# Layer 1's product A X in Strassen's form, and the last image's layer 3 by halves of its positions

## The chip, the cores and the metric

The kernel runs on one core of a Trainium2 chip. TensorE (PE) does the matrix products and transposes into eight PSUM banks of 128 x 512 fp32. VectorE (DVE), ScalarE (ACT) and GpSimd (POOL) do the elementwise work, and SyncE (SP) issues most of the transfers. The metric is the device time of one execution in microseconds (us). Three executions of the kernel before gave a median of 2748.43 us.

## The reference

Two images of 512 channels and 32 x 32 = 1024 positions go through four layers, all in fp32. Layer 0 is deformable attention and an MLP, and is not touched here. The others, in short (X is one image, 512 x 1024):

```
# layer 1: linear attention, then batch norm over both images
K, Q, V = Wq X + bq, Wk X + bk, Wv X + bv      # 8 heads of 64
M   = K V^T per head;  Out = Wo (M^T Q) + bo + X
x   = (Out - mean(Out)) * rsqrt(var(Out) + eps) * gamma + beta
# layer 2: non-local attention, mid = 128
f, g = relu(bn(wf x)), relu(bn(wg x));  h = wh x + bh
z    = softmax(f^T g / sqrt(mid)) h^T;  x = wv z + bv + x
# layer 3: rank-one attention with a channel gate
th, ph, g = theta x, phi x, g x                # one row of 1024 each
y    = softmax(th_i * ph_j, over j) . g        # 1024 values
W_y  = bn(W y + b);  gate = sigmoid(se2 relu(se1 mean(x)))
out  = gate * W_y + x
```

## The kernel before, in words

The channels lie on the partitions in KC = 4 groups of 128. `x` and `x2` are SBUF tiles of 128 x 4 x 2048, where the last axis holds both images. The instructions are written for a Tile scheduler: it puts the instructions of each engine in one order and inserts semaphores where data need them. Instructions given to `tc.keep_in_program_order` keep their written order; of the layers shown here the kernel before uses it nowhere. An engine works through its queue strictly in order, and so does SP's queue of transfers. A PSUM or SBUF pool with `bufs=n` hands out n buffers per tag, and the next user waits for the readers of the one it gets.

**Layer 1 (lines 1205 to 1370).** The layer is linear but for the batch norm, so the kernel folds it. It forms the Gram matrix G = X X^T of each image (lines 1225 to 1254: transposes by PE, copies by DVE and ACT in turn, matmuls), U = G Wv^T (L1270 on), M (L1283 on), R and a bias (L1307 on), and at last A = 512 x 512 for each image (`pa`, L1336, copied to SBUF in L1339). The output is A X + bias1 + X. The weights lie in `lw` (Wq, Wv, Wk, and Wo in two forms). Product A X (lines 1340 to 1354): for each output group o and each 512 positions t, four matmuls over k go into one PSUM bank `pr`, and one DVE instruction (L1352) adds bias1 and X and writes `x2`. This gives 64 matmuls of 128 x 128 by 128 x 512. In the profile an fp32 matmul is two records. Banks come from two pools of four (`dps`, `dpg`).

**Batch norm (lines 1357 to 1370).** For each k: four statistics of 128 x 512 (L1360), an aggregate (L1362), small steps with a square root on ACT (L1365), and a normalisation of 128 x 2048 by DVE (L1370). The statistics of a group can run as soon as its outputs of both images are there; the order of outputs is by o, so groups 0 to 2 are normalised while the product still runs.

**Layer 2 (`l2_fg`, `l2_h`, `l2_attn`, `l2_out`).** For each image: f and g (`pf`, L1385, relu on ACT), h by tiles of 128 positions (`ph`, L1404), then for eight tiles t the scores (L1418, two banks), the row maximum on DVE (L1429), the exponential on ACT (L1432), a scaling on DVE (L1434), eight transposes by PE (L1438) and two copies by ACT (L1439). Then z in two halves (`pz`, L1447) and eight outputs (`pr`, L1458), added to x by DVE (L1466), which also sums each group for the gate's mean.

**Layer 3 (`l3_scores`, `part`, `l3_out`).** The three rows are made by matmuls with 32-wide weights into four partition blocks (`prow`, L1479), copied to SBUF (L1486), and spread over the partitions by matmuls (`pp`, L1494). ACT copies phi and g with their bias to `pg` (L1501), DVE takes the extremes of phi (L1505, L1506), PE turns theta into columns (L1510). For each tile of 128 positions `part` does one exponential on ACT (L1527) and one weighted sum on DVE (L1535). `l3_out` forms y, the gate, spreads y over the partitions (`py`, L1572), and writes each output group: o = 0 by DVE (L1583) then ACT (L1584), the others by ACT (L1586) then DVE (L1587), 1024 positions each, with one store of 512 KB for each (L1588). Image 0's layer 3 is interleaved with image 1's layer 2; image 1's comes after it alone, from a pool of four double banks opened when the others are closed.

## Time and profile before

| what | us |
|---|---|
| median of three executions (2748.21 to 2750.68) | 2748.43 |
| the profiled execution | 2746.91 |
| its span, first to last instruction | 2745.1 |
| its mean granted PE clock, full speed = 1 | 0.995 |
| the product A X, PE | 54.95 |
| last product's end to the first score of layer 2, image 0 | 2565.9 to 2580.0 |
| first score of image 0 to its `pz` | 31.7 |
| last output of layer 2, image 1, on DVE | 2709.4 |
| first exponential of the last layer 3 | 2718.11 |
| last DVE instruction | 2741.0 |

A line of the chain gives a start, a length, an engine, the PSUM or SBUF tile and the source line, with the number of records. A line of groups gives line, engine, operation, output and inputs with their shape, then the total busy time, the mean of one in ns, and the idle time just before with what ended it. A line of windows gives, for a stretch, the busy time and the number of instructions of each engine and the granted PE clock.

### The profile page before, as it was taken

The page shows a single profiled execution, that of the slowest core. Times are in us where ns is not written, and L with a number is a line of the kernel's source. Part 1 is how long each engine was busy: PE and PEld are TensorE (multiplying, and loading weights), DVE is VectorE, ACT ScalarE, POOL GpSimd, SP SyncE. Part 2 cuts the span into 40 slices and gives each one's busy share as a digit, 9 for nine tenths or more (in the row PEclk, how much of TensorE's full clock was granted, in tenths as well). Part 3 has the DMA queues.
Part 4 walks back from the last instruction along what each step waited for, and adds up shares of the span by engine and source line. Part 5 has one row for each costly group of instructions (what it writes and reads, how often), then busy time and mean ns, then how long its engine had stood idle before and what let it go on. Part 6 is the DMA issues. An engine that isn't in the chain of part 4 may idle for free.

```text
span 2745.1 us, 49805 instructions
## 1 busy us (share of the span) xinstructions
PE 2693.7 (98%) x19846; PEld 1003.0 (37%) x19846; DVE 2262.8 (82%) x2465; ACT 1540.5 (56%) x1902; POOL 662.2 (24%) x776
## 2 busy tenths in 40 slices
PE   8999999999999999999999999999999999999996
PEld 4343323333332323333333333333444444454543
DVE  7999999999999999999999999999454445523545
ACT  6676677667668766766766776776221111001244
POOL 0333333333333333333333333333100000000000
PEclk9999999999999999999999999999999999999998
DMA  3777777777777777777787788787310000100001
GB/s 122 166 160 159 164 158 157 165 155 159 158 165 153 162 168 154 164 169 155 165 197 163 156 177 186 157 173 158 85 30 23 16 24 23 77 0 1 0 1 62
DMA packets 145479, 335.15 MB, mean 122 GB/s; under 512 B 22592, under 2 KB 32064, under 8 KB 144480
## 3 DMA queue, kind: packets, MB, share of 16 engines
q0 software_dynamic: 77824, 201.38, 41.3%
q1 hardware_dynamic: 66992, 130.08, 13.4%
q8 instruction: 157, 2.57, 0.4%
q14 instruction: 74, 0.61, 0.1%
q10 hardware_dynamic: 432, 0.51, 0.1%
HBM read 58.99 MB, written 4.46 MB: 23 GB/s over the span
## 4 chain that ended last, share of the span: by engine, by line
PE 93%; DVE 4%; ACT 2%; issue 1%; DMA 0%; ACTq 0%; DVEq 0%; POOL 0%; POOLq 0%
PE ph L615 61%; PE A L1098 4%; PE D L1098 4%; PE C L1098 4%; PE po L1033 2%; PE psim L654 2%; PE pr L1345 2%; PE B L1098 2%; DVE h L348 1%; PE pg L1241 1%; PE pa L1336 1%; PE pz L1447 1%; PE pu L1275 1%; PE pscore L1418 1%; DVE r L630 1%
## 5 line engine op out<-in xcount | busy, mean ns | idle before, releaser
L615 PE MATMUL ph<-h,w2a 128*32 128x512 f32 x16384 | 1792.0, 593 | 3.4 <-ACT r L624 3.3
L624 ACT ACTIVATE r<-ph,sb 128x1024 f32<-128x1024 f32 x1024 | 1142.7, 1116 | 546.5 <-PE ph L615 528.1
L348 DVE CUSTOM_DVE_ANT_1 h<-tab 128x1024 f32<-128x1024 f32 x1024 | 1204.1, 1217 | 13.5 <-PE ph L615 10.4
L615 PEld LDWEIGHTS ph<-h,w2a 128*32 128x32 f32 x16384 | 545.1, 109 | 1203.2 <-issue 805.2
L630 DVE SCALAR_TENSOR_TENSOR r<-r,rel,r 128x1024 f32<-128x1024 f32 x512 | 654.5, 1278 | 12.2 <-ACT r L624 11.6
L645 POOL DMA_DIRECT2D xs<-r x512 | 475.5, 1135 | 190.1 <-PE ph L615 94.4
L633 POOL DMA_DIRECT2D r<-r x256 | 221.4, 865 | 1094.2 <-DVE r L630 913.3
L171 ACT ACTIVATE tab<-tab,vec 128x256 f32<-128x256 f32 x252 | 137.1, 544 | 0.0
L1286 POOL MEMSET M<- 128x512 f32 x2 | 1.0, 518 | 442.6 <-DVE x L1162 442.6
L1138 ACT COPY u<-A 128x512 f32<-128x512 f32 x16 | 9.4, 586 | 146.9 <-PE A L1098 146.9
L1117 ACT ACTIVATE h<-h,vec 128x512 f32<-128x512 f32 x32 | 23.1, 721 | 113.6 <-DVE h L1120 113.6
L654 PE MATMUL psim<-xs,cw 128*32 128x512 f32 x512 | 73.7, 592 | 2.0 <-DMA xs<-r 2.0
L1120 DVE TENSOR_TENSOR h<-C,u 128x512 f32<-128x512 f32 x32 | 22.1, 690 | 47.8 <-PE C L1098 47.4
L1098 PE MATMUL A<-xn,w 128*128 128x512 f32 x128 | 60.3, 593 | 0.8 <-DVE x L1040 0.8
L1098 PE MATMUL C<-hT,w 128*128 128x512 f32 x128 | 60.3, 592 | 0.0
L1098 PE MATMUL A<-h,w 128*128 128x512 f32 x128 | 60.1, 592 | 0.0
L1033 PE MATMUL po<-q,vwo 128*128 128x512 f32 x128 | 58.1, 607 | 0.0
L1345 PE MATMUL pr<-x,A 128*128 128x512 f32 x128 | 55.1, 592 | 0.0
L228 DVE SCALAR_TENSOR_TENSOR acc<-q,vec,acc 128x128 f32<-128x128 f32 (+3 forms) x88 | 46.1, 523 | 0.8
L1158 DVE TENSOR_TENSOR x<-D,x 128x512 f32<-128x512 f32 x32 | 22.1, 690 | 25.9 <-PE D L1098 25.9
L850 ACT ACTIVATE e<-e,den 128x64 f32<-128x64 f32 x128 | 41.7, 337 | 2.0 <-DVE den L846 2.0
L1158 DVE TENSOR_TENSOR x<-C,x 128x512 f32<-128x512 f32 x32 | 22.1, 690 | 24.8 <-PE C L1098 24.8
(287 smaller groups left out, 1763.0 us busy)
## 6 DMA issues: line engine op xcount, KB each, us to landing
r<-r POOLq DMA_DIRECT2D x256, 512.0 KB, 4.8
xs<-r SPq DMA_DIRECT2D x512, 128.0 KB, 2.2
xs<-r POOLq DMA_DIRECT2D x512, 128.0 KB, 4.8
tab<-fd SPq DMA_DIRECT2D x63, 512.0 KB, 6.0
lw<-in_l_w_dram SPq DMA_DIRECT2D x5, 1024.0 KB, 8.9
x<-in_x_dram SPq DMA_DIRECT2D x4, 1024.0 KB, 8.6
w<-in_mlp_w_dram SPq DMA_DIRECT2D x8, 512.0 KB, 4.4
w<-in_mlp_w_dram SPq DMA_DIRECT2D x16, 256.0 KB, 3.2
```

The costliest lines, as they stand in the source:

```text
L171: return nc.scalar.activation(tf, tf if src is None else src[:, :, :, ax, :], AF.Identity, bias=0.0 if ax == 0 else v("L0_conv_cpb_b1"), s ...
L228: pin(nc.vector.scalar_tensor_tensor(dst, src, wt_, dst, ALU.mult, ALU.add))
L348: nc.vector._custom_dve(TENSOR_ADD_SAT, out=h1[:, h], in0=tab[:, j, h, 0, :].unsqueeze(1).to_broadcast([P, 32, 32]), in1=tab[:, j, h, 1, : ...
L615: nc.tensor.matmul(ph[t * 32 : (t + 1) * 32, i, :], lhsT=w2a[:, o], rhs=h1s[2 * p + i][:, h, half * 512 : (half + 1) * 512], start=True, s ...
L624: pin(nc.scalar.activation(r, ph, AF.Relu, bias=sb3[:, o, 1:2]))
L630: pin(nc.vector.scalar_tensor_tensor(r0, r1, rel[:, i : i + 1], r0, ALU.mult, ALU.add))
L633: pin(nc.gpsimd.dma_start(rs[p, 0], rs.pop((p, 2)), accum_op=ALU.add))
L645: pin(nc.gpsimd.dma_start(rs[p][i::2], r[i::2, i, :], accum_op=ALU.add))
L654: nc.tensor.matmul(psims[g, kb][m * 32 : (m + 1) * 32, :], lhsT=cw3[:, 3 - i : 35 - i], rhs=rs.pop(p + m), start=(i == 0), stop=(i == 3), ...
L1033: nc.tensor.matmul(po, lhsT=vwo[:, k * B + t // 2, o * P : (o + 1) * P], rhs=q[:, k, ts_], start=(k == 0), stop=(k == KC - 1),)
L1098: nc.tensor.matmul(banks[bank], lhsT=a[an][k], rhs=b_[bn_][k], start=(i < 4 and k == 0), stop=(k == n - 1), skip_group_check=True,)
L1345: nc.tensor.matmul(pr, lhsT=A[b][:, k, o * P : (o + 1) * P], rhs=x[:, k, ns], start=(k == 0), stop=(k == KC - 1),)
```

## The change

The product A X of each image is done by Strassen's seven products (Winograd's form, which the MLP of layer 0 has already). A and X are cut into 2 x 2 blocks: two groups of 128 channels each way, and 512 positions. `xblocks` holds four difference blocks of X (placed in the second image's part of `x2` and in the weights' room for Wq and Wv), formed ahead of R; `ablocks` holds three sums of A and one difference written in place. `layer_out(b, o)` runs the seven products of two matmuls for output group o of each row block; three banks are added into twice or read and filled again, and DVE (ACT for the first) combines them. The loop order is now image, then o, so groups 0 and 2 are complete in both images before 1 and 3. The batch norm goes by these pairs, normalises each image's half separately, and gives one of the eight pieces (image 0, group 1) to ACT. Layer 2's `l2_fg` and `l2_h` add their groups in the order 0, 2, 3, 1.

The second image's layer 3 leaves `l3_scores`, `part` and `l3_out` and becomes `last`, which also holds the last part of layer 2 (`out_z`, `out_x`) and keeps its written order on every engine. Rows, extremes, mean and outputs go by halves of 512 positions. phi and g get their bias already in the copy of the rows and are read from PSUM; y is spread in two parts; the bias of seven of the eight output pieces is added to x ahead by POOL (`raised`), and DVE then does one instruction for each (`final`); the eighth goes by ACT and POOL (`final_act`). There are eight stores of 256 KB. The scheduler's order of image 0's layer 2 also comes out differently.

The diff, cut to its core (functions not shown, such as `out_z` and `theta`, hold the operations of the kernel before on halves):

```diff
@@ -1304,8 +1304,24 @@
+
+        lo, hi = slice(0, 2), slice(2, 4)
+        places = [x2[:, :, HW:], lw[:, 0:2].rearrange("p i k c -> p (i k c)").rearrange("p (n f) -> p n f", n=4)]
+        xblocks = {}
         for b in both:
-            R = d.tile([P, KC, C], F32, name="R")
+            b11, b21, b12, b22 = (
+                x[:, k, b * HW + t * 512 : b * HW + (t + 1) * 512] for t in range(2) for k in (lo, hi)
+            )
+            t1, t2, t3, t4 = (places[b][:, n].rearrange("p (k f) -> p k f", k=2) for n in range(4))
+            nc.vector.tensor_tensor(t1, b12, b11, ALU.subtract)
+            nc.vector.tensor_tensor(t2, b22, t1, ALU.subtract)
+            nc.vector.tensor_tensor(t4, b21, t2, ALU.subtract)
+            nc.vector.tensor_tensor(t3, b22, b12, ALU.subtract)
+            xblocks[b] = {"11": b11, "21": b21, "22": b22, "T1": t1, "T2": t2, "T3": t3, "T4": t4}
...
-            A[b] = d.tile([P, KC, C], F32, name="A")
+            A[b] = d.tile([P, KC, C], F32, name="A", tag="U")
...
-        for o in range(KC):
-            for t in range(NT // 512):
-                b, ns = t // 2, slice(t * 512, (t + 1) * 512)
-                pr = (dps, dpg)[t % 2].tile([P, 512], F32, name="pr", tag="ps g".split()[t % 2])
-                for k in range(KC):
+        ablocks = {}
+        for b in both:
+            a11, a12, a21, a22 = (A[b][:, k, m] for m in (slice(0, C // 2), slice(C // 2, C)) for k in (lo, hi))
+            s1, s2, s4 = (
+                (wk, won)[b][:, n, :].rearrange("p (k f) -> p k f", k=2) for n in range(3)
+            )
+            differences(a11, a21, a12, a22, s1, s2, s4)
+            ablocks[b] = {"11": a11, "12": a12, "S3": a21, "22": a22, "S1": s1, "S2": s2, "S4": s4}
+
+        def layer_out(b, o):
...
+            def plus(to, t, other):
+                nc.vector.tensor_tensor(to, t, other, ALU.add)
+
+            def final(n, t, other):
+                k = 2 * (int(n[0]) - 1) + o
+                nc.vector.scalar_tensor_tensor(at(n, x2), t, bias1[b][:, k : k + 1], other, ALU.add, ALU.add)
+
+            def c1(t):
+                plus(u, t, u)
+                for n in ("22", "21", "12"):
+                    plus(vs[n], u, at(n, x))
+
+            banks = {n: pool.tile([P, 512], F32, name=f"pr{n}", tag=tag) for n in "ABCD"}
+            for i, (bank, an, bn_, read) in enumerate(
+                [
+                    ("A", "11", "11", lambda t: nc.scalar.copy(u, t)),
+                    ("B", "S2", "T2", c1),
+                    ("C", "S3", "T3", lambda t: plus(vs["22"], t, vs["22"])),
+                    ("D", "S1", "T1", lambda t: final("22", t, vs["22"])),
+                    ("A", "12", "21", lambda t: final("11", t, at("11", x))),
+                    ("C", "22", "T4", lambda t: final("21", t, vs["21"])),
+                    ("D", "S4", "22", lambda t: final("12", t, vs["12"])),
+                ]
+            ):
+                for k in range(2):
                     nc.tensor.matmul(
-                        pr,
-                        lhsT=A[b][:, k, o * P : (o + 1) * P],
-                        rhs=x[:, k, ns],
-                        start=(k == 0),
-                        stop=(k == KC - 1),
-                    )
-                nc.vector.scalar_tensor_tensor(
-                    x2[:, o, ns], pr, bias1[b][:, o : o + 1], x[:, o, ns], ALU.add, ALU.add
-                )
+                        banks[bank],
+                        lhsT=ablocks[b][an][:, k, o * P : (o + 1) * P],
+                        rhs=xblocks[b][bn_][:, k, :],
+                        start=(i < 4 and k == 0),
+                        stop=(k == 1),
+                        skip_group_check=True,
+                    )
+                read(banks[bank])
+        for b in both:
+            for o in range(2):
+                layer_out(b, o)
         x = x2
 
-        for k in range(KC):
-            st = d.tile([P, NT // 512, nc.vector.BN_STATS_DIM], F32, name="st", bufs=2)
-            for t in range(NT // 512):
-                nc.vector.bn_stats(st[:, t, :], x[:, k, t * 512 : (t + 1) * 512])
-            mv = d.tile([P, nc.vector.BN_AGGR_DIM], F32, name="mv", bufs=2)
-            nc.vector.bn_aggr(mv, st.rearrange("p t s -> p (t s)"))
-            sc = d.tile([P, 2], F32, name="sc", bufs=2)
-            nc.vector.tensor_scalar(sc[:, 0:1], mv[:, 1:2], EPS, None, ALU.add)
-            nc.scalar.activation(sc[:, 0:1], sc[:, 0:1], AF.Sqrt)
-            nc.vector.reciprocal(sc[:, 0:1], sc[:, 0:1])
-            nc.vector.tensor_tensor(sc[:, 0:1], sc[:, 0:1], v("L1_conv_gamma", k), ALU.mult)
-            nc.vector.tensor_tensor(sc[:, 1:2], mv[:, 0:1], sc[:, 0:1], ALU.mult)
-            nc.vector.tensor_tensor(sc[:, 1:2], v("L1_conv_beta", k), sc[:, 1:2], ALU.subtract)
-            nc.vector.tensor_scalar(x[:, k, :], x[:, k, :], sc[:, 0:1], sc[:, 1:2], ALU.mult, ALU.add)
+        for ks in ((0, 2), (1, 3)):
+            scs = {}
+            for k in ks:
+                st = d.tile([P, NT // 512, nc.vector.BN_STATS_DIM], F32, name="st", bufs=4)
+                for t in range(NT // 512):
+                    nc.vector.bn_stats(st[:, t, :], x[:, k, t * 512 : (t + 1) * 512])
+                mv = d.tile([P, nc.vector.BN_AGGR_DIM], F32, name="mv", bufs=4)
+                nc.vector.bn_aggr(mv, st.rearrange("p t s -> p (t s)"))
+                sc = scs[k] = d.tile([P, 2], F32, name="sc", bufs=4)
+                nc.vector.tensor_scalar(sc[:, 0:1], mv[:, 1:2], EPS, None, ALU.add)
+                nc.scalar.activation(sc[:, 0:1], sc[:, 0:1], AF.Sqrt)
+                nc.vector.reciprocal(sc[:, 0:1], sc[:, 0:1])
+                nc.vector.tensor_tensor(sc[:, 0:1], sc[:, 0:1], v("L1_conv_gamma", k), ALU.mult)
+                nc.vector.tensor_tensor(sc[:, 1:2], mv[:, 0:1], sc[:, 0:1], ALU.mult)
+                nc.vector.tensor_tensor(sc[:, 1:2], v("L1_conv_beta", k), sc[:, 1:2], ALU.subtract)
+            for b in both:
+                for k in ks:
+                    xs = x[:, k, b * HW : (b + 1) * HW]
+                    if (b, k) == (0, 1):
+                        nc.scalar.activation(xs, xs, AF.Identity, bias=scs[k][:, 1:2], scale=scs[k][:, 0:1])
+                    else:
+                        nc.vector.tensor_scalar(xs, xs, scs[k][:, 0:1], scs[k][:, 1:2], ALU.mult, ALU.add)
...
-            for k in range(KC):
+            for j, k in enumerate((0, 2, 3, 1)):
...
+    def last(b, fp, gp, fps, ps, gps, at2, ht):
+
+        pin = tc.keep_in_program_order
+        ve, pe, act = nc.vector, nc.tensor, nc.scalar
...
+        def row(half, k):
+            if k == 0:
+                prow[half] = gps.tile([P, 512], F32, name=f"prow{half}", tag="l3")
+            pin(
+                pe.matmul(
+                    prow[half][k * 32 : (k + 1) * 32, :], lhsT=w3x[:, k, :], rhs=at(k, half), start=True, stop=True
+                )
+            )
+            if k == KC - 1:
+                pin(act.activation(rows3[:, half, :], prow[half], AF.Identity, bias=b3))
+        def spread(half, i):
+            to_all = c("sel3")[:, i : i + 1].to_broadcast([P, P])
+            pin(pe.matmul(pp[i][:, half, :], lhsT=to_all, rhs=rows3[:, half, :], start=True, stop=True))
+        def turn(half):
+            pt[half] = gps.tile([P, 4, P], F32, name=f"ptl{half}", tag="l3")
+            for t in range(4):
+                pin(pe.transpose(pt[half][:, t, :], rows3[:, half, t * P : (t + 1) * P], ident))
+        def extremes(half):
+            pin(ve.tensor_reduce(ext[:, 0, half : half + 1], pp[0][:, half, :], AX.X, ALU.max))
+            pin(ve.tensor_reduce(ext[:, 1, half : half + 1], pp[0][:, half, :], AX.X, ALU.min, negate=True))
+        def weighted(t):
+            e3 = es.pop(t)
+            g3 = pp[1].rearrange("p a n -> p (a n)")
+            pin(ve.scalar_tensor_tensor(e3, e3, 1.0, g3, ALU.mult, ALU.mult, accum_out=nd[:, 0, t : t + 1]))
+        def mean(half):
+            hs = slice(half * 4, half * 4 + 4)
+            pin(ve.reciprocal(y[:, hs], nd[:, 1, hs]))
+            pin(ve.tensor_tensor(y[:, hs], y[:, hs], nd[:, 0, hs], ALU.mult))
+            py[half] = ps.tile([P, 512], F32, name="pyl", tag="ps")
+            for t in range(4):
+                to_all = y[:, half * 4 + t : half * 4 + t + 1].to_broadcast([P, P])
+                pin(pe.matmul(py[half][:, t * P : (t + 1) * P], lhsT=to_all, rhs=ident, start=True, stop=True))
+        def store(o, half, r):
+            pin(
+                nc.sync.dma_start(
+                    out[b, o * P : (o + 1) * P].rearrange("c h w -> c (h w)")[:, half * 512 : (half + 1) * 512], r
+                )
+            )
+        def raised(o, half):
+            xs = at(o, half)
+            pin(nc.gpsimd.tensor_tensor(xs, xs, aff[:, 1, o : o + 1].to_broadcast([P, 512]), ALU.add))
+        def final(o, half):
+            r = gp.tile([P, 512], F32, name="rl", bufs=6)
+            pin(ve.scalar_tensor_tensor(r, py[half], aff[:, 0, o : o + 1], at(o, half), ALU.mult, ALU.add))
+            store(o, half, r)
+        def final_act(o, half):
+            r = gp.tile([P, 512], F32, name="rl", bufs=6)
+            pin(act.activation(r, py[half], AF.Identity, bias=aff[:, 1, o : o + 1], scale=aff[:, 0, o : o + 1]))
+            pin(nc.gpsimd.tensor_tensor(r, r, at(o, half), ALU.add))
+            store(o, half, r)
...
+        out_z(0)
+        out_z(1)
+        for o in range(KC):
+            out_x(0, o)
+        for o in range(KC):
+            out_x(1, o)
+        for half in range(2):
+            for k in range(KC):
+                row(half, k)
+        spread(0, 0)
+        turn(0)
+        spread(1, 0)
+        turn(1)
+        extremes(0)
+        theta(0)
+        spread(0, 1)
+        spread(1, 1)
+        extremes(1)
+        theta(1)
+
+        pin(ve.tensor_reduce(top, ext, AX.X, ALU.max))
+        pin(ve.tensor_scalar(nm[:, 1, :], th, top[:, 0:1], -1.0, ALU.mult, ALU.mult))
+        pin(ve.scalar_tensor_tensor(nm[:, 0, :], th, top[:, 1:2], nm[:, 1, :], ALU.mult, ALU.min))
+        exponential(0)
...
+        weighted(0)
+        cw = gp.tile([P, KC], F32, name="cw")
+        pin(ve.tensor_tensor(cw, pse[:, 1, 0:KC], v("L3_conv_se2_b"), ALU.add))
+        exponential(1)
+        exponential(2)
+        pin(act.activation(cw, cw, AF.Exp, scale=-1.0))
+        weighted(1)
+        weighted(2)
+        pin(ve.tensor_scalar(cw, cw, 1.0, None, ALU.add))
+        pin(ve.reciprocal(cw, cw))
+        aff = gp.tile([P, 2, KC], F32, name="aff")
+        pin(ve.tensor_tensor(aff, l3s, cw.unsqueeze(1).to_broadcast([P, 2, KC]), ALU.mult))
+        for half in range(2):
+            for o in range(3 + half):
+                raised(o, half)
+        exponential(3)
+        weighted(3)
+        mean(0)
+        for t in range(4, 8):
+            exponential(t)
+        weighted(4)
+        weighted(5)
+        final(0, 0)
+        final_act(3, 0)
+        weighted(6)
+        weighted(7)
+        mean(1)
+        final(1, 0)
+        final(2, 0)
+        for o in range(KC):
+            final(o, 1)
...
-        with tc.tile_pool(name="gpe", bufs=4, space=PSUM) as gps:
-            nd, part = l3_scores(1, gp, gps)
-            for t in range(8):
-                part(t)
-            l3_out(1, gp, gps, nd)
...
+                with tc.tile_pool(name="gpl", bufs=2, space=PSUM) as gps:
+                    last(1, fp, gp, fps, ps, gps, at2, ht)
```

## The prediction

> **What bounds the kernel now.** I began with the page's head, to see which engine is full.
>
> ```profile
> span 2745.1 us, 49805 instructions
> PE 2693.7 (98%) x19846; PEld 1003.0 (37%) x19846; DVE 2262.8 (82%) x2465; ACT 1540.5 (56%) x1902; POOL 662.2 (24%) x776
> ```
>
> TensorE (PE) is busy 98% of the span, so over most of it only fewer matmuls help. The change touches two places, so I read the chain that ended last there (start, length, what).
>
> ```profile
> 2511.11 54.95 PE pr L1345 x128
> 2566.09 0.76 DVE x L1352
> 2566.87 0.70 DVE st L1360
> 2569.10 1.36 DVE x L1370
> 2570.50 9.71 PE pf L1385 x22
> ...
> 2709.47 1.11 PE prow L1479 x8
> 2711.29 1.06 PE prow L1479 x8
> ...
> 2718.11 1.33 ACT e L1527 x2
> 2720.05 9.80 DVE e L1535 x16
> 2730.32 3.60 PE py L1572 x16
> 2733.94 1.29 DVE r L1583
> ...
> 2738.68 1.22 DVE r L1587
> ```
>
> The product A X holds the chain alone for 54.95 us. One matmul is two records, so 64 matmuls cost 0.859 us each. Behind it the chain passes for 4.4 us over VectorE (DVE), but PE hides nearly all of that with matmuls of layer 2 that need only the groups already normalised. From 2709 on PE is no longer the bound: the last image's layer 3 is a chain of DVE, ACT and a few matmuls. Busy time by stretch (product, boundary, tail) says the same:
>
> ```profile
> core 0: us, PE busy (x) PEld busy (x) DVE busy (x) ACT busy (x) POOL busy (x), PEclk, DMA share, GB/s
> 2511.00:2566.00 55.00, 55.00 (x130) 24.39 (x129) 28.45 (x51) 2.48 (x5) 0.00 (x0) 1.00 0.00 0
> 2566.00:2580.00 14.00, 13.84 (x33) 5.88 (x32) 3.84 (x9) 2.53 (x4) 0.00 (x0) 1.00 0.00 0
> 2701.00:2746.00 45.00, 19.70 (x80) 9.27 (x78) 26.03 (x56) 18.30 (x28) 0.00 (x0) 0.75 0.12 47
> ```
>
> DVE is half idle beside the product, and that is the room the extra additions have. Their prices are in the rows of the groups (busy, mean ns of one):
>
> ```profile
> L1352 DVE SCALAR_TENSOR_TENSOR x<-pr,bias,x 128x512 f32<-128x512 f32 x16 | 12.0, 748 | 27.4 <-PE pr L1345 27.4
> L1360 DVE BATCH_NORM_STATS2 st<-x 128x6 f32<-128x512 f32 x16 | 11.1, 694 | 0.5
> L1587 DVE TENSOR_TENSOR r<-r,x 128x1024 f32<-128x1024 f32 x6 | 7.0, 1220 | 4.6 <-ACT r L1586 4.6
> L1286 POOL MEMSET M<- 128x512 f32 x2 | 1.0, 518 | 442.6 <-DVE x L1162 442.6
> ```
>
> **The product: −6.9 us.** Seven block products of two matmuls, two output groups, two images make 56 matmuls; eight fewer at 0.859 us. Per output group PE needs 14 × 0.859 = 12.0 us; DVE has five additions (about 0.69 us), four finals (0.75) and four statistics (0.69), 9.2 us, so it keeps up and no PSUM bank should hold PE back.
>
> **The blocks of X: +0.9 us.** Eight subtractions of 128x1024 at 1.22 us each go onto DVE ahead of or among layer 1's small products; the scheduler puts image 0's first two ahead of DVE's copies for the Gram matrix and image 1's one ahead of the evacuation of the last U group. Both are work that PE waits for. I walk these as +0.35 (the rest of 2.44 us lies under the end of the MLP) and +0.6 (between 0.45 and 0.8, because of the four DVE steps before M). The other subtractions, and the six for A, lie under matmuls that need none of them. Without that cover each would cost 1.22 us.
>
> **The boundary to layer 2: +2.3 us.** Here a wait is enlarged. Count from the start of the last output group; its seven products end at 1.72, 3.43, ... 12.02. DVE must first do the sum of B (3.43 to 4.18), two reciprocals, three additions and the addition of C (7.2), four scale steps (7.8), a final (8.55), two scale steps (8.85), a statistic (9.54), then four normalisations of groups 0 and 2 (0.75 each) with two finals between (14.05), the last final (14.8), three statistics (16.85), two aggregates and the small steps, with a turn over ACT's square root (19.3), and the normalisation of group 3 (20.1), while ACT does group 1 (1.17 us, 20.6). PE runs out earlier: after 12.02 it has six pf matmuls (5.15 us) and two short ph ones, to 17.6. It idles to about 20.1, 2.5 us, where it idled 0.16 before. Behind the waiting matmul stands all of layer 2. The cost could be as low as 1.2 us (DVE 1 us ahead of my walk) or as high as 3.6.
>
> The Trainium skill, "TensorE: Matmul & The Clock Gate", Part 1 "What's actually happening", says that about 3.4 us of idle put the array on half clock until some 3.4 us of busy time have passed. The trace agrees in kind: 16 py records take 3.60 us after 11.2 us of idle, against 1.8 (0.67 + 1.12) for image 0's. With the row alone 2.5 us of stall cost 2.3; by the rule a stall grown past 3.4 us would add about 1.7 us of lost work, some +5 in all. I take the first, and keep the second for a rival.
>
> **Layer 2 of image 0: +1.0 us.** The scheduler orders the score matmuls and the transposes of the softmaxed tiles otherwise than before: the second half of the last score tile now stands behind two tiles' transposes. Before, the stretch from the first score to pz is 31.7 us; my walk with the same durations gives up to 33.9; three ph matmuls done earlier give 0.65 back. Bounds 0 and +2.2, I take the middle. Image 1's layer 2 keeps its order.
>
> **The tail: −6.0 us.** Four steps, against the chain above.
> 1. Rows. Half 0's four row matmuls no longer wait for the last layer-2 outputs, and half 1's no longer wait for the copy of half 0's rows (PE waited 0.85 and 0.75 us). Half 1's end moves from 2712.36 to 2709.45 + 1.06 = 2710.5. The copy with bias (0.69), the spread, and four reductions (0.69 each), which no longer wait for ACT's copies, lead to the exponent's bias at 2716.6, against 2718.02: −1.4.
> 2. Eight weightings. Before, the first waits for a copy of g (2720.05). Now it starts at about 2718.0; eight at 1.23 to 1.28 us, small steps (0.6), the first half's mean (0.35) and one final (0.75) between them: end at 2729.95.
> 3. Mean and y. Second mean 0.4; eight py records at half clock 1.8 (half of 3.60): 2732.2. DVE does two finals of half 0 beside them (to 2731.85).
> 4. Four finals of 0.75: 2735.2, where ACT and DVE alternated over 128x1024 pieces to 2741.03 before: −5.8. The last store has 256 KB in place of 512; its landing took 2.6 to 2.9 us before; I give it −0.2.
>
> Eight stores in place of four stand on SP's queue in fixed order, 0.33 us each to issue: hidden by the finals' 0.75 spacing, unless one waits for POOL.
>
> **What the tail needs of POOL.** Seven bias additions of 128x512 start when the gate is ready (about 2722.5), and an eighth finishes piece (3,0), whose store stands second in SP's queue, ahead of six others. The trace has no POOL addition. Nearest row: the memset, 0.52 us. The Trainium skill, "GPSIMD Engine Reference", section 3.1, speaks against the change: it gives two-input elementwise as some 2.6 cycles per element, 4497 ns at 2048 fp32, by which I estimate 1.12 us for 512. By the row the eighth ends at 2722.5 + 4.1 = 2726.6, by the rule at 2731.5. The last store must be issued at 2735.3 behind six others at 0.33, so the eighth may end at 2733.3: both are covered, up to 1.35 us each. I take 1.12, since an addition has two inputs. Beyond 1.35 the tail grows by 8 us per us.
>
> **Sum.** −6.9 + 0.9 + 2.3 + 1.0 − 6.0 = −8.7. The profiled execution took 2746.91 with a span of 2745.1 (1.8 around it); span 2736.4, run 2738.2. The median of the runs is 1.5 above the profiled one, so I add the difference to the median: 2748.43 − 8.7 = 2739.7, said as 2740.
>
> **The rivals.** 0.2% is 5.5 us, about what a measurement of this kernel can tell from no change.
> - *DVE does better than walked.* The boundary costs 1.2, layer 2's order nothing: −11 us, 2737. For it: DVE is half idle in the product's stretch. Against it: its steps at the boundary are one serial chain.
> - *Strassen's gain is eaten.* The boundary crosses the clock gate (+5) and layer 2 takes +2.2: −6.9 + 0.9 + 5 + 2.2 = +1.2, and with the tail −4.8: 2743.6. For it: 0.9 us more of lateness suffices. It ends on the edge of no change.
> - *The tail brings nothing.* POOL takes about 2.1 us per addition: the eighth ends at 2739.3, six stores and a landing later the span's end stands where it was, leaving −2.7: 2745.7.
> - *Slower: POOL is the bound.* The same place, dearer. If all before the tail gives −2.7, the kernel is 5.5 us slower once eight additions take 8.2 us more than in the last case, about 3.1 us each; with about 6 us for loading code ahead of the first addition ("GPSIMD Engine Reference", section 2.1 "Instruction dispatch", gives that for a first call; no run here shows it, and a setup instruction of POOL's stands in front of the adds) 2.4 us each suffice. 2754 to 2760. Against it: POOL is idle from 2511 on, so setup can run far ahead.
>
> **How the numbers follow.** Likeliest 0.50 (own range 2737 to 2743), better 0.17, eaten 0.16, no tail 0.11, slower 0.06. Faster by over 0.2% (below 2742.9): 0.50 + 0.17 + half of the eaten case = 0.75, less 0.02 for the likeliest case's edge; same 0.21; slower 0.06. The range leaves out the slower case and the better one's far end: 2735 to 2749.
>
> **What would show it.** Product rows: 112 records in about 48 us with no PE idle. Idle before the pf row (released by DVE or ACT's normalisation) of 1.2 to 3.6 us; the granted clock there at 1.0. First score to pz of 31.7 to 33.9. Tail: first exponential 1.4 us nearer to the last layer-2 output, POOL additions of at most 1.3 us, no final with a releaser on POOL, last DVE instruction 25.8 us after that output rather than 31.6. Wrong it would be made by a product row with waits for DVE, by a boundary over 4 us, or by finals that wait for POOL.

## The result

The changed kernel takes 2738.04 us (median of five executions, 2736.91 to 2738.80) against 2748.74 for the kernel before on the same chip (five executions; the 2748.43 given ahead of the prediction is the median of the first three of them). The ratio is 0.9961, with a 95% interval of 0.9951 to 0.9972: about 10.7 us or 0.39% faster. 2740 was predicted, with 2735 to 2749 as the range. The head of the page of the changed kernel (span, then busy time by engine):

```profile
span 2735.1 us, 49862 instructions
PE 2688.7 (98%) x19830; PEld 1000.6 (37%) x19830; DVE 2286.2 (84%) x2509; ACT 1538.1 (56%) x1901; POOL 671.1 (25%) x784
```

The span is 10.0 us shorter and PE's busy time only 5.0. So half of the gain is time in which PE had nothing to do. The chain that ended last, in the changed kernel (start, length, what):

```profile
2512.29 1.72 PE prA L1400 x4
...
2561.03 0.66 DVE x L1380
2561.69 1.78 DVE st L1420 x3
...
2564.89 1.25 ACT x L1434
2566.19 0.71 PE ph L1470 x4
2566.90 8.59 PE pf L1451 x20
2575.48 0.86 PE pscore L1484 x2
...
2607.80 15.43 PE pz L1513 x32
...
2706.24 1.90 PE prow L1704 x16
...
2713.95 1.30 ACT e L1734 x2
...
2726.93 2.09 PE pyl L1757 x8
...
2731.18 0.66 DVE rl L1773
```

The stretches of the product, the boundary, the end of image 0's layer 2 and the start of its z (busy time by engine, with the granted PE clock):

```profile
core 0: us, PE busy (x) PEld busy (x) DVE busy (x) ACT busy (x) POOL busy (x), PEclk, DMA share, GB/s
2512.00:2560.00 48.00, 48.00 (x113) 21.28 (x112) 37.74 (x67) 4.51 (x8) 0.00 (x0) 1.00 0.00 1
2560.00:2575.00 15.00, 14.54 (x39) 6.74 (x38) 7.02 (x21) 3.91 (x6) 0.00 (x0) 1.00 0.00 1
...
2604.00:2607.80 3.80, 1.07 (x9) 1.10 (x10) 1.48 (x4) 1.61 (x3) 0.00 (x0) 0.99 0.01 2
2607.80:2612.00 4.20, 4.20 (x7) 1.65 (x7) 0.00 (x0) 0.67 (x2) 0.00 (x0) 0.60 0.02 4
```

The product keeps PE full, and the boundary holds 0.46 us of idle. The surprise is in the third and fourth row: near the end of image 0's layer 2 PE works 1.07 of 3.8 us, and then the clock is granted at 0.60 while z starts. PE's longest wait between the first score and z (who waited for whom: us in total, times, longest), before and then in the changed kernel:

```profile
PE pt L1438 <- DVE e L1434: 1.8, 2, 1.3
```

```profile
PE pt L1504 <- DVE e L1500: 2.7, 1, 2.7
```

The untouched layer 0 ends at a different time in every profile (the last MLP matmul between 2386.97 and 2389.66 us over those read here). I therefore count from that end: 2386.97 before and 2387.41 after. By that count the changed kernel gains 358.13 − 347.69 = 10.44 us, close to the 10.7 of the medians. By part:

| stretch | before | after | change | predicted |
|---|---|---|---|---|
| MLP's end to the product's start | 124.14 | 124.88 | +0.74 | +0.9 |
| product | 54.95 | 48.07 | −6.88 | −6.9 |
| wait at the boundary | 0.16 | 0.46 | +0.30 | +2.3 |
| rest, to image 0's first z matmul | 45.67 | 46.98 | +1.31 | +1.0 |
| image 0's z | 13.73 | 15.43 | +1.70 | 0 |
| from there to the last output of layer 2 | 83.8 | 83.8 | 0 | 0 |
| last output of layer 2 to the end | 35.7 | 28.1 | −7.6 | −6.0 |

The changes add up to −10.4, against −8.7 predicted.

### The profile page after: what moved, and what is told of

Read it like the earlier page. It is cut to its first block, busy times and chain, and to the rows that moved or that the text cites. A ratio compares the mean times of both kernels' runs of the same rounds, so it can differ in the third digit from the quotient of the medians.

```text
span 2735.1 us, 49862 instructions
## 1 busy us (share of the span) xinstructions
PE 2688.7 (98%) x19830; PEld 1000.6 (37%) x19830; DVE 2286.2 (84%) x2509; ACT 1538.1 (56%) x1901; POOL 671.1 (25%) x784
## 4 chain that ended last, share of the span: by engine, by line
PE 92%; DVE 4%; ACT 2%; issue 1%; DMA 0%; DVEq 0%; POOL 0%; ACTq 0%; POOLq 0%
PE ph L615 62%; PE A L1098 4%; PE D L1098 4%; PE C L1098 4%; PE psim L654 2%; PE B L1098 2%; PE po L1033 2%; DVE h L348 1%; PE pg L1241 1%; PE pa L1352 1%; PE pu L1275 1%; PE pscore L1484 1%; PE pz L1513 1%; DVE r L630 1%; PE pz L1686 1%
## 5 line engine op out<-in xcount | busy, mean ns | idle before, releaser
L348 DVE CUSTOM_DVE_ANT_1 h<-tab 128x1024 f32<-128x1024 f32 x1024 | 1205.3, 1219 | 13.6 <-PE ph L615 10.4
L1769 POOL TENSOR_TENSOR x<-x,aff 128x512 f32<-128x512 f32 x7 | 7.0, 1034 | 328.8 <-DVE aff L1833 328.8
L1158 DVE TENSOR_TENSOR x<-C,x 128x512 f32<-128x512 f32 x32 | 22.1, 690 | 24.8 <-PE C L1098 24.8
```

What stands on the lines that cost most here:

```text
L348: nc.vector._custom_dve(TENSOR_ADD_SAT, out=h1[:, h], in0=tab[:, j, h, 0, :].unsqueeze(1).to_broadcast([P, 32, 32]), in1=tab[:, j, h, 1, : ...
L1158: nc.vector.tensor_tensor(to, t, to, ALU.add)
```

## The experiments

By their medians most of these runs cannot be told from the changed kernel: the intervals of their ratios overlap its 0.9951 to 0.9972. What a run is worth by part is therefore read from its trace, from the MLP's end on.

**The two halves of the change alone.** First only the new `last`, then only the product, the batch norm and the order of layer 2.

```diff
 e1: layer 1, l2_fg and l2_h of the kernel before;  last(1, ...) at the end
 e2: the changed layer 1, l2_fg and l2_h;  at the end
-    with tc.tile_pool(name="gpl", bufs=2, space=PSUM) as gps:
-        last(1, fp, gp, fps, ps, gps, at2, ht)
+        l2_out(1, fp, ps, at2, ht)
+    with tc.tile_pool(name="gpe", bufs=4, space=PSUM) as gps: ...
```

> The kernel before with the new last layer 3 alone; product, batch norm and layer-2 order as before. Theory (the tail and the product add up): up to the last image's z matmuls nothing moves, and from the last layer-2 output to the end the tail takes 28.0 us as in the changed kernel (35.6 before), so the span is 2745.1 - 7.6 = 2737.5, within 0.6. Rival (the tail is only worth what the prediction said, and the rest of the changed kernel's gain comes from the product's side): 2739.1.

> The changed kernel with the old last layer 3: Strassen's product, the batch norm by pairs and the new order in layer 2. Theory: the product's matmuls end 5.7 us earlier than before, layer 2 of image 0 loses 3.3 of it (a wait of 2.7 us before the last transposes, and z at 15.4 us in place of 13.7), so the span is 2745.1 - 2.4 = 2742.7. Rival (the disturbed order of layer 2 is brought about by the pinned tail): no such wait, and 2739.4.

Measured: the tail alone 2739.98 us, ratio 0.9973 (0.9963 to 0.9983). From the MLP's end its span is 350.53 us, 7.60 under the kernel before, and the tail is 28.1 us long. The product alone: 2744.87 us, ratio 0.9990 (0.9983 to 0.9997); 355.52 from the MLP's end, 2.61 under. The halves add up to 10.2 of the 10.4 us. z in the chain of the run with the product alone:

```profile
2609.35 15.37 PE pz L1513 x32
```

z is slow here too, so it comes with the product's half. From first score to the end of z the kernel before and the tail-only kernel need 45.4 us, both kernels with the new product 47.8. Of the 6.9 us that Strassen's form saves, 2.6 arrive.

**Is it the clock?** Eight matmuls that nobody reads, laid into the wait before the last transposes.

```diff
+    def filler(t, psh, fg):
+        if t == 7:
+            fill = psh.tile([P, P], F32, name="fill", tag="h")
+            for i in range(8):
+                nc.tensor.matmul(fill, lhsT=ident, rhs=fg[:, 0, i * P : (i + 1) * P], start=True, stop=True)
-    ... lambda t: l2_h(0, t, ht, psh, "h"))
+    ... lambda t: (l2_h(0, t, ht, psh, "h"), filler(t, psh, fg)))
```

> The changed kernel with eight matmuls of 128x128 whose result nobody reads (about 1.8 us), placed in the 2.7 us wait ahead of the last transposes of image 0's layer 2. Theory (the wait lowers the granted clock, and that makes z slow): the clock in the first 4 us of z is 1.0 instead of 0.60, z takes 13.7 instead of 15.4 us, span 2733.4. Rival (z is slow for another reason, such as its operands arriving late): z stays at 15.4, span 2735.1 or longer.

Measured: 2736.99 us, ratio 0.9960 (0.9945 to 0.9975). Chain of that run:

```profile
2576.66 0.86 PE pscore L1484 x2
...
2608.98 13.74 PE pz L1519 x32
```

The first 4.2 us of its z as a window, in the columns used above:

```profile
2608.98:2613.18 4.20, 4.20 (x11) 1.81 (x11) 0.00 (x0) 0.67 (x2) 0.00 (x0) 1.00 0.00 0
```

First score to z is 32.32 us as in the changed kernel, the clock is granted at 1.00 in place of 0.60, and z is back at 13.74. Work that does nothing bought 1.69 us against that one profile, so the slow z is the clock's doing. The same holds over all profiles read here: with the 2.7 us wait z took 14.21 to 15.43 us (five profiles), without it 13.73 to 13.83 (five). From the MLP's end the whole run gains only 0.86: its tail is 0.8 us longer, as the four small matmuls of the gate take 1.76 us in place of 1.05, the gate's first addition stands ahead of the second weighting on DVE, and DVE waits. The same four took from 1.05 to 1.86 us in the ten profiles with the new tail, without an edit to them. That is the lowered clock again, at another place: over these matmuls it was granted at 0.54 here, at 1.00 in the changed kernel. Why it comes in some profiles and not in others stays open.

**The order of image 0's layer 2.** Everything given to the engines in a written order, the scores of tile t + 2 ahead of the transposes of tile t.

```diff
+        for t in range(2):
+            scores(t); hmat(t); top(t)
+        for t in range(8):
+            scale(t)
+            if t + 2 < 8:
+                scores(t + 2)
+            turn(t)
+            if t + 2 < 8:
+                top(t + 2); hmat(t + 2)
```

> The changed kernel with image 0's layer 2 in a written order: scores of tile t+2 ahead of the transposes of tile t on PE, and DVE and ACT in the matching order. Theory (the order left by the scheduler costs the wait, and the wait costs the clock): the longest PE wait between the first score and z is under 1.5 us, z takes 13.7 us, first score to z under 31.5 us (32.3 now), span 2731 to 2732.5. Rival (the softmax chain sets this stretch in any order): the wait comes back elsewhere, the stretch stays at 32, span 2733.5 or more.

Measured: 2736.16 us, ratio 0.9957 (0.9942 to 0.9971). First score to z is 31.50 us, z 13.83, the longest waits 1.5 (behind the first exponential) and 1.3. So the mechanism holds, and the size missed: 2.4 us are won up to the end of z, but the wait and the stretch only reached their expected limits, and the tail fell into the long form (1.86 us for the gate's matmuls). From the MLP's end 1.7 us are left of the 2.6 to 4.1 expected.

**The boundary made late.** Four more statistics in DVE's chain.

```diff
+                if k == 3:
+                    st2 = d.tile([P, NT // 512, nc.vector.BN_STATS_DIM], F32, name="st2", bufs=1)
+                    for t in range(NT // 512):
+                        nc.vector.bn_stats(st2[:, t, :], x[:, k, NT - 512 :])
+                    nc.vector.tensor_copy(st[:, 3, :], st2[:, 3, :])
                 mv = d.tile([P, nc.vector.BN_AGGR_DIM], F32, name="mv", bufs=4)
```

> The changed kernel with four more statistics (and one small copy) in DVE's chain before group 3 is normalised, about 2.4 to 3 us, with no other use. Theory (DVE's chain of scale steps sets the start of layer 2, with no slack left): PE's wait at the boundary grows one for one, from 0.46 to about 3 us. If a wait of that length takes the clock, as the 2.7 us wait in layer 2 seems to, the pf matmuls behind it take about 1.7 us longer, so +4.5 us in all; if only the layer-2 wait did so, +2.7. Rival (there is slack at the boundary that the reading of the trace missed): under +1 us.

Measured: 2741.19 us, ratio 0.9978 (0.9969 to 0.9986); 352.51 from the MLP's end, 4.8 over the changed kernel. PE's waits of that run (engine, line, waited for: us in total, times, longest), and its windows behind them:

```profile
PE pt L1509 <- DVE e L1505: 2.7, 1, 2.7
PE ph L1475 <- ACT x L1439: 2.0, 1, 2.0
PE pf L1456 <- DVE x L1441: 1.0, 1, 1.0
...
2562.00:2570.00 8.00, 5.72 (x18) 2.71 (x16) 7.42 (x24) 1.54 (x3) 0.00 (x0) 1.00 0.00 0
2570.00:2575.00 5.00, 4.24 (x6) 1.84 (x7) 1.42 (x2) 0.46 (x1) 0.00 (x0) 0.66 0.00 0
```

The wait grew from 0.46 to 3.0 us, nearly as much as the added work takes (four statistics about 0.65 us apart and the copy, some 2.7): there is no hidden slack. Then the clock fell to 0.66 and the 20 pf records took 10.55 us in place of 8.59, another 1.96. The rest of the 4.8 us nearly cancels: first score to z is 0.9 us longer, z is 1.2 shorter (14.21), and the tail is 0.6 longer.

**POOL made slow.** Two memsets ahead of each addition of the tail.

```diff
+            pin(nc.gpsimd.memset(idle_, 0.0))
+            pin(nc.gpsimd.memset(idle_, 0.0))
             pin(nc.gpsimd.tensor_tensor(xs, xs, aff[:, 1, o : o + 1].to_broadcast([P, 512]), ALU.add))
```

> The changed kernel with two memsets of 128x512 (0.5 us each) ahead of each of POOL's eight additions in the tail, so about 2.05 us for each piece in place of 1.03. The prediction's rival says that at 2.1 us each the tail brings nothing. Theory (store (3,0) holds the six behind it): the eighth addition ends at about 16.5 us after POOL's start, against 8.2 now, and with about 2 us of slack the last store goes out 6 us later, span 2741. Rival (each final waits only for its own piece, and the stores are not held): the last DVE instruction moves by 3 us at most, span 2738.

Measured: 2744.72 us, ratio 0.9990 (0.9983 to 0.9996). Lines of its timeline (start, length, engine, what, in brackets the idle time before and who ended it):

```profile
2731.32 0.75 DVE L1776 SCALAR_TENSOR_TENSOR rl<-pyl,aff,x 128x512 f32<-128x512 f32 x1 [0.46 <-POOL x L1772]
...
2734.35 1.26 POOL L1784 TENSOR_TENSOR rl<-rl,x 128x512 f32<-128x512 f32 x1
2737.76 0.75 DVE L1776 SCALAR_TENSOR_TENSOR rl<-pyl,aff,x 128x512 f32<-128x512 f32 x1 [5.68 <-DMA out_dram<-rl]
```

The tail is 35.8 us, as long as before the change (35.7): this is the rival "the tail brings nothing", at the price per addition that the prediction gave it. The eighth addition ends 7.7 us later than in the changed kernel, counted from the last output of layer 2, and so does the kernel: one for one. The path is not the finals' own bias pieces (0.46 us of waiting) but the store. Piece (3,0) is the second store and is late, so the stores behind it stand, and with six buffers the last final must wait 5.68 us for one of theirs.

**Four edits together.** X's blocks on POOL, h moved into the waits of layer 2, small matmuls that keep PE busy in the tail, one more piece by ACT and POOL.

```diff
-            nc.vector.tensor_tensor(t1, b12, b11, ALU.subtract)      # and t2, t4, t3
+            nc.gpsimd.tensor_tensor(t1, b12, b11, ALU.subtract)
...
+            warm(t, (2, 3, 3, 8)[t - 4])        # n matmuls ones-by-ident behind exponential t
...
+        final_act(3, 1)
+        for o in range(KC - 1):
             final(o, 1)
```

> The changed kernel with four edits: X's blocks formed on POOL; image 0's layer 2 in the written order of the earlier run with h of tiles 2 to 7 moved into its first and last waits; in the tail small matmuls that nobody reads keep PE busy before y is spread; the gate's first addition on DVE stands behind the second weighting, and piece (3,1) goes by ACT and POOL like (3,0). Theory, each by its own stretch: end of the MLP to the product's start 124.1 (124.9 now); first score to z under 29.5 us (32.3 now, 31.5 in the earlier run) and z at 13.7; spreading the second half of y 1.0 us (2.07 now); last output of layer 2 to the end 1.6 us shorter; in sum about 6 us under the changed kernel. Rival for the clock in the tail (the matmuls that keep PE busy delay y or the weightings more than they save): the tail at 28.0 us or longer.

Measured: 2737.35 us, ratio 0.9960 (0.9946 to 0.9974). Most of the expectation failed: from the MLP's end the run is 0.9 us under the changed kernel, not 6. MLP's end to product is 125.7 us, not 124.1: POOL's subtractions made it worse. The timeline there shows why:

```profile
2388.42 0.75 DVE L1162 SCALAR_TENSOR_TENSOR x<-vs,vec,x 128x512 f32<-128x512 f32 x1
...
2389.51 2.36 POOL L1318 TENSOR_TENSOR x<-x 128x1024 f32<-128x1024 f32 x1 [441.26 <-PE D L1098]
2390.13 2.28 DVE L1162 SCALAR_TENSOR_TENSOR x<-vs,vec,x 128x512 f32<-128x512 f32 x1
```

The same DVE instruction, both tensors in SBUF, takes 0.75 us alone and 2.28 beside POOL's subtraction; it ends half a microsecond after POOL does. First score to z was 31.0 us, not under 29.5: near its start PE still waited twice for DVE's additions to h (0.4 us each) and near its end 1.4 us for a scaling, though z ran at 13.74. In the tail the second spread did fall to 0.91 us. But the sixteen matmuls ahead of it ran to 2728.11 where y was ready at 2727.08, and the second piece by ACT and POOL came only at 2731.16, with its store behind it: 29.5 us from the last output of layer 2 to the end, so the rival was right.

**A version from what was learnt.** X's blocks back on DVE; the row maximum ahead of h's addition; half of z's matmuls in the last waits of layer 2, which they can be because the first half of the positions needs only tiles 0 to 3; ten small matmuls in place of sixteen; y's reciprocal in PSUM.

```diff
+            if t == 5:
+                early_z((0, 1))
+            if t == 6:
+                early_z((2, 3))
+            if t == 7:
+                early_z((4, 5, 6, 7))
...
+            inv = pse[:, 1, 8 + half * 4 : 12 + half * 4]
-            pin(ve.reciprocal(y[:, hs], nd[:, 1, hs]))
-            pin(ve.tensor_tensor(y[:, hs], y[:, hs], nd[:, 0, hs], ALU.mult))
+            pin(ve.reciprocal(inv, nd[:, 1, hs]))
+            pin(ve.tensor_tensor(y[:, hs], inv, nd[:, 0, hs], ALU.mult))
```

> The changed kernel with X's blocks on DVE as they are; image 0's layer 2 in a written order that takes each row maximum ahead of the addition to h and lays eight of the sixteen z matmuls into the waits of the last tiles; in the tail ten small matmuls that nobody reads in place of sixteen between the two spreads of y, the gate's first addition behind the second weighting, and the reciprocal for y written to PSUM. Theory (PE can be kept full in layer 2): first score to the first output matmul of layer 2, which is 47.8 us in the changed kernel (32.3 and 15.4), is 43 us or less; (the product for y waits for POOL because both its operands lie in SBUF) that product takes 0.2 us in place of 0.53; (y is spread at half clock) the second spread takes 1.0 us in place of 2.07; in sum 5 to 6.5 us under the changed kernel, 2731.5 to 2733. Rival (the softmax chain of DVE and ACT holds layer 2): 46 us, and the whole gains 2 us.

Measured: 2733.79 us, ratio 0.9942 (0.9929 to 0.9956); 4.95 us under the changed kernel from the MLP's end, where 5 to 6.5 were expected. First score to the end of z, as windows, in the changed kernel and then in this one:

```profile
2575.50:2623.20 47.70, 43.89 (x187) 26.03 (x187) 18.23 (x32) 20.49 (x35) 0.00 (x0) 0.96 0.00 1
```

```profile
2577.60:2620.40 42.80, 42.16 (x193) 25.91 (x193) 18.62 (x32) 20.28 (x35) 0.00 (x0) 1.00 0.00 1
```

PE now is full there, at clock 1.00. The second product for y with POOL's additions beside it, in the changed kernel and then in this one:

```profile
2719.84 7.02 POOL L1769 TENSOR_TENSOR x<-x,aff 128x512 f32<-128x512 f32 x7 [328.77 <-DVE aff L1833]
...
2726.35 0.53 DVE L1753 TENSOR_TENSOR y<-y,nd 128x4 f32<-128x4 f32 x1
...
2726.82 1.26 POOL L1779 TENSOR_TENSOR rl<-rl,x 128x512 f32<-128x512 f32 x1
```

```profile
2717.10 7.01 POOL L1855 TENSOR_TENSOR x<-x,aff 128x512 f32<-128x512 f32 x7 [323.78 <-DVE aff L1932]
...
2723.62 0.16 DVE L1839 TENSOR_TENSOR y<-psel,nd 128x4 f32<-128x4 f32 x1
```

The expected values came in layer 2 and for y (0.16 us), and nearly for the second spread (1.16 us in place of 2.07). But the tail as a whole did not shorten: 28.2 us. Counted from the last output of layer 2 the last DVE instruction ended 0.8 us earlier, but the end came 0.9 us later behind it. That left a question: what sets the end?

**The place of POOL's eighth addition.**

```diff
-        for half in range(2):
-            for o in range(3 + half):
-                raised(o, half)
+        for o, half in ((0, 0), (1, 0), (2, 0), (0, 1), (1, 1)):
+            raised(o, half)
...
         final_act(3, 0)
+        raised(2, 1)
+        raised(3, 1)
```

> The changed kernel with one edit: POOL's addition for piece (3,0) stands behind five of its seven bias additions instead of behind all seven. Theory (the end is set by the stores: the second of eight waits for this addition, and the six behind it wait in SP's queue, while the memory then takes about 380 GB/s): in the changed kernel, in the earlier best version and in the run with the slow POOL the end comes 7.0 us after this addition, whatever DVE does; it now ends 2 us earlier, the stores no longer wait for it, and the last output of layer 2 to the end shrinks from 28.1 to about 27.2 us, then limited by DVE's finals. Rival (the finals on DVE set the end already): 28.1 us, no change.

> The best version so far with the same edit. Theory: there the finals came 0.8 us earlier than in the changed kernel and the end did not, since the stores waited; with the store free, last output of layer 2 to the end 26.5 us (28.2 in the best version so far), median about 2732. Rival (the finals set the end): 28.2 us.

Measured: in the changed kernel, 2738.13 us, ratio 0.9963 (0.9949 to 0.9976), and 28.0 us of tail: no change, so there the rival was right. A part of this is a side effect: the moved additions now stand beside the second product for y, which took 0.77 us in place of 0.53, and the finals end 0.24 us later. In the best version, 2731.21 us, ratio 0.9939 (0.9926 to 0.9951), and 26.6 us of tail in place of 28.2, as the theory had it. The ratios of the two best versions overlap; their traces differ by 1.6 us from the MLP's end, all of it in the tail. The memory's rate over the tail in GB/s, in 40 slices of 2715 to 2750, for the changed kernel and then the last one:

```profile
GB/s 0 0 0 0 0 0 0 0 0 0 9 286 14 0 0 19 377 382 391 379 379 171 0 0 0 0 0 0 0 0 0 0 0 0 0 0 0 0 0 0
```

```profile
GB/s 0 0 0 0 0 0 9 208 91 19 281 314 372 379 375 358 0 0 0 0 0 0 0 0 0 0 0 0 0 0 0 0 0 0 0 0 0 0 0 0
```

In the changed kernel one store goes out, then nothing for about 2 us, then seven stores at some 380 GB/s: 7 × 0.262 MB are 4.8 us. Two limits lie within about 0.3 us of each other in it, the finals (25 us, then about 3 to the end) and the addition for piece (3,0), which ends 7.0 us ahead of the end (as it does, within 0.1 us, in the run with the slow POOL and in the first version from what was learnt). Moving the one shows the other. Only where the finals come earlier does the order of the stores decide.

## Why the prediction was right

The time was right by 2 us, and in part by luck: the boundary was charged 2.0 us too much, and layer 2 of image 0 with its z 2.0 us too little. These two cancel; the 1.6 us that the tail brought beyond its term are what is left.

- *The product, −6.9:* −6.88, in full and without a wait for DVE. *The blocks of X, +0.9:* +0.74.
- *The boundary, +2.3:* +0.3. The step that failed is the walk of DVE, which charged each instruction the mean of its row. From the start of the last output group to group 3's normalisation it gave 19.3 us; DVE took 16.6. Instructions that wait for nothing start 0.66 us after one another where the row says 0.75, 0.60 where it says 0.69 (the chain above: a final in 0.66, three statistics in 1.78), and 0.07 to 0.1 where a small one says 0.15. Over thirty-odd instructions in a row that makes the 2.7 us; 1.0 of it lies in the last aggregates and small steps with their turn over ACT, 1.4 us in place of 2.45. The mechanism was right, as the late boundary shows: it is one serial chain, and what was added to it came out as waiting. The 0.46 us that were left are a wait for ACT's piece (1.24 us for group 1), not for DVE's group 3, with which the walk ended the wait.
- *Layer 2 of image 0, +1.0:* +1.3, of that three ph matmuls done earlier counted. The prediction had the culprit, the second half of the last scores behind two tiles' transposes. It missed what follows: a wait of 2.7 us in one piece, and 1.7 us of slow z. It weighed a loss of clock at the boundary, where the wait proved short, and not here; and by the some 3.4 us of idle that the Trainium skill, "TensorE: Matmul & The Clock Gate", Part 1, speaks of, a wait of 2.7 us would have been charged nothing. The term was missing from the sum, not mis-sized; the run with the filler shows it.
- *The tail, −6.0:* −7.6. Step 1: −1.8 in place of −1.4. Step 2: the weightings end 19.2 us after the last output of layer 2, not 20.5, again by starts 1.14 us apart where rows of 1.23 to 1.28 were charged. Step 3: the second spread took 2.07, not 1.8, and the product for y 0.53. Step 4: the finals end at 24.8, not 25.8. The last store: −0.8, not −0.2.
- *POOL:* 1.03 us for an addition of 128x512, against the 1.12 estimated from the Trainium skill, "GPSIMD Engine Reference", section 3.1, and 0.52 by the row of the memset. The page was the better guide. No final waited for POOL, and at 2.05 us each the tail brought nothing, as the rival said. But the slack was mis-sized: the prediction let an addition take 1.35 us, because it charged each of the six stores behind the eighth only 0.33 us to issue. The runs show 7.0 us from that addition to the end, so at 1.03 us each there was already none: in the changed kernel the stores end about 0.3 us after the finals alone would let them.

## What to carry to other kernels

A serial chain on DVE is to be walked with the distance between starts, seen where the trace shows instructions back to back, and not with the mean length in the rows; over thirty-odd instructions that was 2.7 of 19.3 us. A gain of PE time has to be followed to the next place where an engine stands idle: here a new order two stages later ate 3.0 of 6.9 us, by its wait and by the clock that the wait cost. Where several stores stand in one queue, one that is ready late holds those behind it: making it ready earlier brought 1.6 us in the best version (issuing it last was not tried). A change that moves only one of two nearly equal limits shows nothing until the other moves too.

## What was not expected of the hardware

- *The clock fell behind waits of 2 to 3 us.* A wait of 2.7 us, with PE busy 1.07 of 3.8 us around it, was followed by a granted clock of 0.60 over 4.2 us, and waits of 2.0 and 1.0 us with short work between them by 0.66 over 5. With waits of up to 1.5 us in layer 2, z took 13.73 to 13.83 us. In five profiles with the 2.7 us wait (the changed kernel, the product alone, and the runs with a late boundary, a slow POOL and a moved addition) the next z took 15.43, 15.37, 14.21, 14.36 and 15.18 us, so the price was 0.5 to 1.7 us and varied between executions of the same instructions. The Trainium skill, "TensorE: Matmul & The Clock Gate", Part 1, speaks of some 3.4 us of idle; here less was enough.
- *DVE and POOL exclude each other on some instructions.* A DVE instruction with two SBUF tensors took 2.28 us in place of 0.75 beside a POOL subtraction. A product of 128x4 with both operands in SBUF took 0.53 us in the changed kernel and ended with the addition that POOL was in (2726.88 against 2726.86). In the run with the moved addition it took 0.77 (2728.85 against about 2728.82), and in the run with four edits the first product took 0.96 (2721.53 against about 2721.48). Started within 0.1 us of the end of an addition, as the first product of the changed kernel was, it took 0.16 us, and so it did in the middle of an addition once one operand was in PSUM (2723.62 above). The weightings and finals, which have one operand in PSUM, showed no such delay: 1.21 and 0.74 us beside POOL. This fits the Trainium skill, "SBUF — State Buffer", section "Who interferes with whom", which says that two SBUF inputs on DVE contend with a POOL instruction that reads SBUF.
